# Third layer's experts: the order of the output additions, of the weight differences and of the small operations

## The chip, the cores and the metric

The kernel runs on one core of one Trainium2 chip. The metric is the device time of one launch in microseconds (us); the median of three runs stands for the kernel. Engines are called by the profile's names: PE is TensorE, DVE is VectorE, ACT is ScalarE, POOL is GpSimd, SP is the engine whose queue issues most of the DMAs.

## The reference, cut to what matters

The program is four layers on a picture of 256 channels and 64 x 64 positions (4096 tokens). The change lies in the end of the last layer, the mixture of experts:

```python
def _L3_ffn_ref(x, Wg, bg, W1, b1, W2, b2):
    xf = x.reshape(-1, D)
    gate_logits = xf @ Wg + bg
    top_w, top_i = jax.lax.top_k(gate_logits, TOP_K)
    top_w = jax.nn.softmax(top_w, axis=-1)
    w_dense = jnp.sum(jax.nn.one_hot(top_i, E, dtype=xf.dtype) * top_w[..., None], axis=1)
    out = jnp.zeros_like(xf)
    for e in range(E):
        h = jax.nn.gelu(xf @ W1[e] + b1[e], approximate=False)
        out = out + w_dense[:, e:e + 1] * (h @ W2[e] + b2[e])
    return out.reshape(B, L, D)
```

There are 8 experts, each token goes to 2 of them, the width is 256 and the hidden width 1024; everything is float32.

## The kernel before, in words

Tokens are sorted by expert into rows of a DRAM array `xs`, and the experts then work on tiles of 256 rows of one expert. `expert_tiles` (L2336) runs 36 such tiles, numbered 0 to 35 here. Tiles 0 to 19 (list "A") come from the first 3584 tokens and can start before the last block of 512 tokens has been routed; tiles 20 to 35 come from list "B".

Work of one tile *i*:

- `first` (L2373): the hidden layer. Eight products of 128 x 256 (`f_h_ps`, each four matmul records in the profile, so 32 a tile), each followed by a GELU on ACT (L2380). A PSUM buffer holds two products, and there are three of them, so a product can wait for an earlier GELU.
- `turn` (L2369): PE transposes the next tile's rows, DVE copies them (`f_xT`, L2308). The next tile's `first` needs them.
- `sums` (L2411): four DVE operations on halves of h (`f_hs`, L2419 to L2422). `sides` (L2400): four POOL operations on halves of the second weights (`f_wt`, L2408). Both feed a product by seven smaller products in place of eight (Strassen's scheme in Winograd's form).
- `second` (L2448) for the tile *before* (i - 1): `seven` (L2425) makes the seven products, first `ya`'s (two PSUM buffers) and `yb`'s (one), in the order ya, yb, yb, ya x3, yb. ACT copies one product (`f_u`, L2441), five DVE additions join them (L2442 to L2446), the sixth adds the bias (`f_y`, L2452), ACT multiplies by the router's weight (L2459, two operations), and POOL issues two indirect DMAs that scatter the rows to `ys` (L2460).
- `where` (L2396, with `expert_where`, L2287): eight or nine DVE operations of 128 x 2 elements (L2290 to L2301) that work out where tile i + 1's rows go and their weights. They are the "small operations" of the title.

Inside the loop, in the kernel before, the order of issue is: loads of later tiles (SP), `first`, `sides(i)`, hs[2], slot "hs", hs[0], `turn(i + 1)`, hs[1], hs[3], `where(i + 1)`, slot "turn", `second(i - 1)`, slot "end". The slots are filled from a table, `plan` (`put`, L2884): steps of the routing of the last block and of the tile list B, the check `limits3` (L2946), and for late tiles the reading back and transposing of finished output blocks. Each slot's step issues all that it holds on whatever engine: the layer norm of the last block (four DVE operations, L240, and a small POOL copy, L2055) at (2, "hs"), its transposes `part["turn"]` (L2057; PE, then an ACT or DVE copy, L2061) at (2, "turn") and (2, "end"), the logits (PE) at (3, "turn"), and so on.

What sets the order on each engine: while `written` (L2336, L2515) is in force, PE, DVE and POOL keep the order of the code (`manual_schedule`); ACT and SP are ordered by the library's scheduler with its own costs. When no entry of `plan` before tile 20 is left, only DVE keeps the code's order, and the scheduler orders PE and POOL too. In the kernel before this switch comes after tile 11 (its "hs" slot holds `limits`). I call tiles up to the switch "planned" and those after it "free".

The list A is made in `attn3` (L2580) near the end of the attention, in five steps of a generator `list_tiles` (L2120), spread over three of the attention's steps: `next(lists)` twice, twice and once (L2863 to L2868).

Of the kernel before, what the change touches and what calls it, by code (L numbers as in the profile page):

```python
# [26 lines left out]
TPB = NB // P  # L27
# [57 lines left out]
def bc(ap, axis, n):  # L85

    ap = ap.unsqueeze(axis)
    shape = list(ap.shape)
    shape[axis] = n
    return ap.to_broadcast(shape)  # L90


class Net:
# [2242 lines left out]
    def expert_tiles(self, S, order, wp, ps, early, pre, written):  # L2336
# [28 lines left out]
        def extra(i, slot):  # L2365
            for f in plan.pop((i, slot), ()):
                f()
# [32 lines left out]
        def sides(w2):  # L2400

            if L == 2:
                return None
            wt = wp.tile([P, 4, KH // 2, P], F32, tag="wt", name="f_wt", bufs=2)
            b = w2[:, : KH * C].rearrange("p (i m j n) -> p i m j n", i=2, j=2, n=P)
            for out, x, y in ((0, b[:, 0, :, 1], b[:, 0, :, 0]), (1, b[:, 1, :, 1], wt[:, 0]), (2, b[:, 1, :, 1], b[:, 0, :, 1]),
                              (3, b[:, 1, :, 0], wt[:, 1])):
                nc.gpsimd.tensor_tensor(wt[:, out], x, y, ALU.subtract)  # L2408
            return wt
# [12 lines left out]
                lambda: op(hs[:, 3], a[:, 1, :, 0], hs[:, 1], ALU.subtract),  # L2422
            )

        def seven(h, hs, w2, wt, y):  # L2425

            a = h.rearrange("p (i m) (j n) -> p i m j n", i=2, n=P)
            b = w2[:, : KH * C].rearrange("p (i m j n) -> p i m j n", i=2, j=2, n=P)

            pa = ps.tile([P, 4, P], F32, tag="ya", name="f_ya_ps", bufs=2)  # L2430
            pb = ps.tile([P, 4, P], F32, tag="yb", name="f_yb_ps")
            for out, x, z in (
                (pa[:, 0], a[:, 0, :, 0], b[:, 0, :, 0]), (pb[:, 2], a[:, 1, :, 0], b[:, 1, :, 0]), (pb[:, 1], a[:, 1, :, 1], wt[:, 3]),
                (pa[:, 2], hs[:, 0], wt[:, 0]), (pa[:, 1], hs[:, 1], wt[:, 1]), (pa[:, 3], hs[:, 2], wt[:, 2]), (pb[:, 0], hs[:, 3], b[:, 1, :, 1]),
            ):
                self.mm(out, [(x[:, m], z[:, m]) for m in range(KH // 2)])
            u1 = wp.tile([P, P], F32, tag="u1", name="f_u1")
            u2 = wp.tile([P, P], F32, tag="u2", name="f_u2")
            u = wp.tile([P, 2, P], F32, tag="u", name="f_u")
            flat = y.rearrange("p k (j n) -> p (k j) n", n=P)  # L2440
            nc.scalar.copy(u1, pa[:, 0])  # L2441
            nc.vector.tensor_tensor(flat[:, 0], u1, pb[:, 2], ALU.add)  # L2442
            nc.vector.tensor_tensor(u2, u1, pa[:, 1], ALU.add)
            nc.vector.tensor_tensor(u, pa[:, 2:4], bc(u2, 1, 2), ALU.add)
            nc.vector.tensor_tensor(flat[:, 3], u[:, 1], pa[:, 2], ALU.add)
            nc.vector.tensor_tensor(flat[:, 1:3], u, pb[:, 0:2], ALU.add)  # L2446

        def second(i, h, hs, w2, wt, at, wgt):  # L2448
            y = wp.tile([P, NI, C], F32, tag="y", name="f_y")
            if L == 3:  # L2450
                seven(h, hs, w2, wt, y)
                nc.vector.tensor_tensor(y, y, bc(w2[:, KH * C :], 1, NI), ALU.add)  # L2452
            else:
                p = ps.tile([P, NI, C], F32, tag="y", name="f_y_ps", bufs=2)
                for k in range(NI):
                    self.mm(p[:, k, :], [(h[:, m, k * P : (k + 1) * P], w2[:, m * C : (m + 1) * C]) for m in range(KH)])
                nc.vector.tensor_tensor(y, p, bc(w2[:, KH * C :], 1, NI), ALU.add)
            for k in range(NI):
                nc.scalar.mul(y[:, k, :], y[:, k, :], wgt[:, k : k + 1])  # L2459
                nc.gpsimd.indirect_dma_start(  # L2460
                    out=self.ys_parts[(i % 4) * NI + k], in_=y[:, k, :], in_offset=None,
                    out_offset=bass.IndirectOffsetOnAxis(ap=at[:, k : k + 1], axis=0),
                )
# [17 lines left out]
            to[0] = where(0, xs[0])  # L2481
        done = None
        free = not pre
        for i in tiles:
            if i + ahead_x <= tiles[-1]:
                xs[i + ahead_x] = rows(i + ahead_x)
            if i + ahead <= tiles[-1]:
                ws[i + ahead] = weights(i + ahead)
            w1, w2 = ws.pop(i)
            h = first(i, turned.pop(i), w1, not free)  # L2490
            hs, add = sums(h)
            now = (i, h, hs, w2, sides(w2)) + to.pop(i)
            for f in add[:1]:
                f()
            extra(i, "hs")
            for f in add[1:2]:
                f()
            if i < tiles[-1]:
                if i + 1 not in turned:
                    turned[i + 1] = turn(xs[i + 1])  # L2500
                for f in add[2:]:
                    f()
                to[i + 1] = where(i + 1, xs[i + 1])
                xs.pop(i)
            else:
                for f in add[2:]:
                    f()
            extra(i, "turn")
            if done is not None:
                second(*done)  # L2510
            extra(i, "end")
            done = now
            if not free and not any(k < pre["free"] for k, _ in plan):
                free = True
                written.close()  # L2515
                written.enter_context(self.tc.manual_schedule(engines={mybir.EngineType.DVE}))
# [63 lines left out]
    def attn3(self, t, S, out, limits):  # L2580
# [6 lines left out]
        with (  # L2587
# [28 lines left out]
            if True:  # L2616
# [230 lines left out]
                with tc.manual_schedule(engines={ET.PE, ET.Pool}):  # L2847
                    steps = iter(())
                    for g in range(first, G + LAG):
                        if g < G:  # L2850
                            scores(g)
                        values(g - LAG)
                        if g + 3 < G:
                            fetch(g + 3)
                        b, j = divmod(g - LAG, NPAIR)
                        if b > 0:
                            if j < TPB:
                                finish(b - 1, j)
                            elif j == TPB:
                                steps = routing((b - 1) * TPB, TPB, self.route)  # L2860
                            elif j % 2 == 0 or b == NBLK - 1:
                                next(steps, None)
                            if b == NBLK - 1 and j == TPB + 5:  # L2863
                                lists = self.list_tiles(S, keep, bank, "A", FULL)
                            if b == NBLK - 1 and j in (TPB + 5, TPB + 6):
                                next(lists)
                                next(lists)
                            if b == NBLK - 1 and j == TPB + 7:  # L2868
                                next(lists)
                                one = lambda shape, tag: keep.tile([P] + shape, F32, tag=tag, name="f_" + tag, bufs=1)  # L2870
                                tab = S["A"]["tab"], 0
                                pre = {"pool": keep, "x": self.expert_rows(*tab, one([NI, CX], "x")),
                                       "w": self.expert_weights(3, *tab, lambda: one([16 * P + 8], "w1"), lambda: one([9 * C], "w2"))}
                            if b == NBLK - 1 and j == NPAIR - 2:
                                pre["xT"] = self.expert_turn(pre["x"], bank().rearrange("p (k n) -> p k n", k=2), one([2, MT], "xT"))
                                tl = lambda tag, dt=F32: keep.tile([P, NI], dt, tag="e" + tag, name="f_" + tag, bufs=1)
                                pre["to"] = self.expert_where(S["A"], 0, pre["x"], tl)
# [10 lines left out]
                put(0, i, lambda i=i: (finish(last, i), part["stats"]([i])))  # L2888
            put(1, "turn", part["root"])
            put(2, "hs", part["scales"], part["norm"])  # L2890
            put(2, "turn", lambda: part["turn"](0))
            put(2, "end", lambda: part["turn"](1))
            put(3, "turn", part["logits"], part["top"], part["exp"])
            put(3, "end", part["weigh"], part["count"])
            put(4, "turn", part["place"], part["find"])
            put(4, "end", lambda: part["scatter"](range(2)))
            put(5, "end", lambda: part["scatter"](range(2, TPB)))
            put(5, "turn", go)
            put(6, "hs", go)
            put(7, "hs", go)  # L2900
            put(8, "hs", go)
            put(9, "turn", go)
            put(11, "hs", limits)
            ys = {}
            channels = out.rearrange("(m p) n -> p m n", p=P)

# [289 lines left out]
```

## Time and profile before

| what | us |
|---|---|
| median of three runs | 3430.52 |
| lowest, highest | 3427.38, 3432.81 |
| the profiled execution, its own time | 3429.62 |
| its span, first to last instruction | 3427.9 |
| planned tiles 2 to 12 (first matmul of tile 2 to that of tile 13) | 2884.68 to 3055.84: 171.16 |
| free tiles 13 to 30 | 3055.84 to 3314.57: 258.73 |
| tiles 31 to 35, with transposes of output among them | 3314.57 to 3392.99: 78.42 |

A tile's time is read off as the distance between the starts of its first `f_h_ps` matmul (from tile 31 on, of the output transpose that stands ahead of it) and that of the next tile. In the order of the tiles from 2 to 12 these are 19.75, 15.39, 14.04, 13.83, 13.60, 15.45, 14.89, 13.89, 13.60, 13.60 and 23.12 us; tiles 13 to 30 take 14.37 us each on average; 31 to 34 take 15.77 each and 35 takes 15.33. Times of the profile are microseconds from the start of the span. A line of the timeline has start, length, engine, line of the code, operation, what it writes and reads, shapes and count; in brackets stands the idle time of that engine just before, and who ended it.

### The profile page before, as it was taken

Reading aid. Unit: us, or ns where it says so; the run is one execution under the profiler, and the core shown is the slowest. Engines: PE = TensorE matmul, PEld = TensorE weight load, DVE = VectorE, ACT = ScalarE, POOL = GpSimd, SP = SyncE. Lnnn points to the kernel's source line nnn. Section 1 sums busy time; section 2 is a strip of 40 time slices with the busy share of each in tenths; the row PEclk is TensorE's granted clock in tenths of the full one; section 3 lists DMA queues with packets and bytes.
Section 4 is the critical chain, followed back from the end, with each engine's and each line's share of the span. In section 5 each row is a group of like instructions: output and inputs, shape, how many; then the busy total and the mean of one; then the engine's idle time right before and its main releaser. Section 6 shows DMA issues by size and latency. Waiting matters only on the chain. (4 is left out here: it accounts for less than half of the span.)

```text
span 3427.9 us, 66058 instructions
## 1 busy us (share of the span) xinstructions
PE 3111.8 (91%) x25682; PEld 2327.6 (68%) x25682; DVE 2353.5 (69%) x5332; ACT 1327.0 (39%) x2558; POOL 1455.1 (42%) x1316
## 2 busy tenths in 40 slices
PE   6779999999977899897959789999999999999997
PEld 3443444344436888666748667888888888988886
DVE  8885767577754677796646576777777776765564
ACT  4444344444425666243434353222222223323332
POOL 2028788788843555443434443000000013555552
PEclk9889999999989999998869899999999999999999
DMA  1145556521134222100129663233332234555564
GB/s 71 43 115 142 163 153 169 130 68 52 49 114 114 68 68 72 52 1 2 50 103 288 211 224 131 86 94 103 97 102 91 88 93 180 187 189 194 194 237 158
DMA packets 241689, 407.01 MB, mean 119 GB/s; under 512 B 78353, under 2 KB 152850, under 8 KB 231890
## 3 DMA queue, kind: packets, MB, share of 16 engines
q1 hardware_dynamic: 212866, 347.55, 32.6%
q0 software_dynamic: 13056, 35.93, 2.8%
q10 hardware_dynamic: 15440, 19.16, 1.7%
q8 instruction: 207, 3.39, 0.4%
q14 instruction: 120, 0.98, 0.1%
HBM read 287.07 MB, written 111.30 MB: 116 GB/s over the span
## 5 line engine op out<-in xcount | busy, mean ns | idle before, releaser
L776 ACT COPY l_sc<-l_s 128x384 f32<-128x384 f32 (+1 forms) x632 | 304.1, 533 | 453.5 <-PE l_s L769 442.4
L781 DVE TENSOR_TENSOR l_sm<-l_s,mask 128x256 f32<-128x256 f32 (+2 forms) x628 | 308.0, 552 | 89.8 <-PE l_s L769 88.7
L152 PE MATMUL f_h_ps<-f_xT,f_w 128*128 128x256 f32 x1440 | 345.5, 387 | 22.8 <-ACT f_h L2380 19.2
L2112 POOL DMA_INDIRECT xs<-f_room,f_to x64 | 64.4, 1007 | 644.0 <-DVE a_e L2737 476.9
L152 PEld LDWEIGHTS f_h_ps<-f_xT,f_w 128*128 128x128 f32 x1440 | 264.0, 191 | 82.5 <-ACT f_h L2380 32.7
L769 PE MATMUL l_s<-l_q,l_k 32*128 32x256 f32 (+3 forms) x2944 | 270.6, 453 | 0.0
L2769 ACT ACTIVATE a_e<-a_e 128x512 f32<-128x512 f32 x256 | 156.4, 631 | 250.2 <-DVE a_e L2739 229.2
L786 POOL TENSOR_TENSOR l_sm<-l_sc,mask 128x768 f32<-128x768 f32 (+1 forms) x116 | 202.6, 1754 | 87.8 <-ACT l_sc L776 87.7
L2460 POOL DMA_INDIRECT ys<-f_y,f_at x144 | 142.3, 988 | 193.6 <-ACT f_y L2459 144.4
L1156 DVE TENSOR_TENSOR l_pr<-l_vk,l_w_ps 128x1280 f32<-128x1280 f32 x128 | 186.7, 1483 | 54.3 <-PE l_acc_ps L1160 35.2
L2380 ACT ACTIVATE f_h<-f_h_ps,f_w 128x256 f32<-128x256 f32 x360 | 157.7, 469 | 164.0 <-PE f_h_ps L152 134.2
L769 PEld LDWEIGHTS l_s<-l_q,l_k 32*128 32x128 f32 x2944 | 132.5, 183 | 115.2 <-issue 66.8
L1160 PE MATMUL l_acc_ps<-ident,l_pr 128*128 128x128 f32 x1600 | 198.5, 278 | 6.3 <-POOL l_pr L1151 6.3
L1160 PEld LDWEIGHTS l_acc_ps<-ident,l_pr 128*128 128x128 f32 x1600 | 185.1, 144 | 12.9 <-POOL l_pr L1151 7.8
L790 POOL TENSOR_TENSOR l_sm<-l_sc,mask 128x256 f32<-128x256 f32 (+1 forms) x220 | 185.2, 871 | 14.6 <-ACT l_sc L776 13.9
L2408 POOL TENSOR_TENSOR f_wt<-f_w 128x512 f32<-128x512 f32 x72 | 93.3, 1310 | 187.9 <-PE f_ya_ps L152 158.4
L2750 PE MATMUL a_sa_ps<-a_q,a_kt 128*128 128x256 f32 x512 | 156.9, 388 | 17.8 <-DVE a_u L2755 15.9
L2754 ACT COPY a_u<-a_sa_ps 128x256 f32<-128x256 f32 x128 | 47.6, 372 | 292.4 <-PE a_sa_ps L2750 290.0
L2750 PE MATMUL a_sa_ps<-a_qt,a_kt 128*128 128x256 f32 x512 | 153.5, 382 | 0.0
L815 PE MATMUL l_b_ps<-l_sm,l_v 128*32 128x256 f32 (+2 forms) x2176 | 153.5, 372 | 0.0
L786 POOL TENSOR_TENSOR l_sm<-l_sc,mask_c 128x768 f32<-128x768 f32 (+1 forms) x64 | 121.0, 1906 | 39.8 <-ACT l_sc L776 39.2
L2789 PE MATMUL a_ob_ps<-a_et,a_vs 128*128 128x256 f32 x512 | 132.2, 381 | 0.0
(620 smaller groups left out, 7325.5 us busy)
## 6 DMA issues: line engine op xcount, KB each, us to landing
a_kt<-a_kd SPq DMA_DIRECT2D x128, 512.0 KB
f_w<-in_f_w SPq DMA_DIRECT2D x36, 1152.0 KB
f_w<-in_f_w SPq DMA_DIRECT2D x36, 1028.0 KB
xs<-zero SPq DMA_DIRECT2D x8, 4160.0 KB
l_vk<-vt SPq DMA_DIRECT2D x180, 128.0 KB
f_x<-xs SPq DMA_DIRECT2D x72, 260.0 KB
f_w<-in_f_w SPq DMA_DIRECT2D x36, 384.0 KB
l_rcp<-l_recd SPq DMA_DIRECT2D x48, 256.0 KB
```

The lines of the kernel that those rows point to most:

```text
L152: self.nc.tensor.matmul(out, lhsT, rhs, start=(i == 0), stop=(i == len(pairs) - 1))
L769: nc.tensor.matmul(s[pair, j][:, at : at + m, :], key(hp), qs[hp], start=(z == 0), stop=(z == len(pieces) - 1))
L776: nc.scalar.copy(sc[:, j], s[1, j])
L781: nc.vector.tensor_tensor(to(pair, j, kind, at), pick(s[pair, j], kind, which), mask, ALU.mult)
L786: nc.gpsimd.tensor_tensor(out[:, :, at, :], of[:, :, which, :], bc(mask, 1, 2), ALU.mult)
L790: nc.gpsimd.tensor_tensor(to(1, j, kind, at), pick(sc[:, j], kind, which), mask, ALU.mult)
L815: nc.tensor.matmul(out, pieces[z][1](hp), self.halves(sms[pair][:, j], wide)[:, of + skip * lo : of + skip * (hi - 1) + 1 : skip], start=n ...
L1156: nc.vector.tensor_tensor(pr, vk, bc(held["w"][:, j, dy], 3, D), ALU.mult)
L1160: nc.tensor.matmul(acc[:, m, j, :], pf[:, dx, m * P : (m + 1) * P], self.ident, is_transpose=True, start=(j == 0 and dy == 0 and dx == 0 a ...
L2380: nc.scalar.activation(h[:, m, :], p[:, m % 2, :], AF.Gelu, bias=w1[:, 2 * hidden + m : 2 * hidden + m + 1])
L2750: mm = lambda out, i, right: nc.tensor.matmul(out, A[i], right, start=True, stop=True)
L2769: nc.scalar.activation(e[:, i : i + 3 : 2], e[:, i : i + 3 : 2], AF.Exp, scale=1.0 / 16.0)
```

## The change

Three things are moved; no operation is added or removed.

1. In `seven`, the addition that reads `yb` (`flat[:, 0]`) comes after the two that read only `ya`.
2. The weight differences of tile i + 1 (`sides`) are issued inside `second(i - 1)`, right after its seven products, instead of those of tile i at the start of iteration i.
3. `where(i + 1)` comes right after hs[2] instead of after hs[3].

With them the plan is spread anew (steps come later, most by one tile), and the list A's steps are shared 3, 1, 1 instead of 2, 2, 1. The switch from planned to free now comes after tile 12.

```diff
-        def seven(h, hs, w2, wt, y):
+        def seven(h, hs, w2, wt, y, beside):
...
                 self.mm(out, [(x[:, m], z[:, m]) for m in range(KH // 2)])
+            beside()
...
             nc.scalar.copy(u1, pa[:, 0])
-            nc.vector.tensor_tensor(flat[:, 0], u1, pb[:, 2], ALU.add)
             nc.vector.tensor_tensor(u2, u1, pa[:, 1], ALU.add)
             nc.vector.tensor_tensor(u, pa[:, 2:4], bc(u2, 1, 2), ALU.add)
+            nc.vector.tensor_tensor(flat[:, 0], u1, pb[:, 2], ALU.add)
...
-            now = (i, h, hs, w2, sides(w2)) + to.pop(i)
+            now = (i, h, hs, w2, wts.pop(i)) + to.pop(i)
             for f in add[:1]:
                 f()
+            if i < tiles[-1]:
+                to[i + 1] = where(i + 1, xs[i + 1])
             extra(i, "hs")
             for f in add[1:2]:
                 f()
-            if i < tiles[-1]:
-                if i + 1 not in turned:
-                    turned[i + 1] = turn(xs[i + 1])
-                for f in add[2:]:
-                    f()
-                to[i + 1] = where(i + 1, xs[i + 1])
-                xs.pop(i)
-            else:
-                for f in add[2:]:
-                    f()
+            if i < tiles[-1] and i + 1 not in turned:
+                turned[i + 1] = turn(xs[i + 1])
+            for f in add[2:]:
+                f()
             extra(i, "turn")
-            if done is not None:
-                second(*done)
+
+            def beside():
+                if i < tiles[-1]:
+                    wts[i + 1] = sides(ws[i + 1][1])
+
+            if L == 2 or done is None:
+                beside()
+            if done is not None:
+                second(*done, beside)
...
-                                next(lists)
-                                next(lists)
+                                for _ in range(3 if j == TPB + 5 else 1):
+                                    next(lists)
...
-            put(2, "turn", lambda: part["turn"](0))
-            put(2, "end", lambda: part["turn"](1))
-            put(3, "turn", part["logits"], part["top"], part["exp"])
-            put(3, "end", part["weigh"], part["count"])
-            put(4, "turn", part["place"], part["find"])
-            put(4, "end", lambda: part["scatter"](range(2)))
-            put(5, "end", lambda: part["scatter"](range(2, TPB)))
-            put(5, "turn", go)
-            put(6, "hs", go)
+            put(2, "end", lambda: part["turn"](0))
+            put(3, "turn", lambda: part["turn"](1))
+            put(3, "end", part["logits"])
+            put(4, "hs", part["top"])
+            put(4, "turn", part["exp"])
+            put(5, "hs", part["weigh"], part["count"])
+            put(5, "turn", part["place"])
+            put(5, "end", part["find"], lambda: part["scatter"](range(2)))
+            put(6, "end", lambda: part["scatter"](range(2, TPB)))
+            put(6, "turn", go)
             put(7, "hs", go)
             put(8, "hs", go)
-            put(9, "turn", go)
-            put(11, "hs", limits)
+            put(9, "hs", go)
+            put(10, "turn", go)
+            put(12, "hs", limits)
```

`go` is one step of list B's generator, `limits` the check of `limits3`.

## The prediction

> **What bounds the kernel now.** I read the page's first parts (PE is 91% busy, clock 0.952), then PE's waits in the experts' stretch, then the timeline of single tiles. PE's own waits between 2870 and 3410 us:
>
> ```profile
> PE f_h_ps L152 <- ACT f_h L2380: 19.2, 24, 6.4
> PE tr_ps L251 <- ACTq L2333: 8.5, 1, 8.5
> PE f_h_ps L152 <- issue: 3.0, 3, 1.7
> PE a_q_ps L2060 <- DVE f_room L240: 2.9, 3, 1.0
> ```
>
> PE makes the tiles' pace, and it waits for the GELUs that free its PSUM buffers. Where it doesn't wait a tile takes 13.60 us (tiles 10 and 11). That is the floor; the timeline shows four kinds of excess over it.
>
> A free tile (its first matmul at T = 3199.58):
>
> ```profile
> 3198.94 2.50 POOL L2408 TENSOR_TENSOR f_wt<-f_w 128x512 f32<-128x512 f32 x2 [6.56 <-PE f_ya_ps L152]
> 3198.94 0.27 ACT L2441 COPY f_u<-f_ya_ps 128x128 f32<-128x128 f32 x1 [5.38 <-PE f_ya_ps L152]
> 3199.84 0.29 DVE L2442 TENSOR_TENSOR f_y<-f_u,f_yb_ps 128x128 f32<-128x128 f32 x1 [2.02 <-PE f_yb_ps L152]
> 3200.04 0.28 DVE L2443 TENSOR_TENSOR f_u<-f_u,f_ya_ps 128x128 f32<-128x128 f32 x1
> ...
> 3201.39 2.94 POOL L2408 TENSOR_TENSOR f_wt<-f_w,f_wt 128x512 f32<-128x512 f32 x2
> 3201.47 1.74 DVE L2452 TENSOR_TENSOR f_y<-f_y,f_w 128x512 f32<-128x512 f32 x1
> ...
> 3203.25 0.91 ACT L2459 ACTIVATE f_y<-f_y,f_wgt 128x256 f32<-128x256 f32 x2 [1.26 <-DVE f_y L2452]
> ...
> 3204.06 1.19 ACT L2380 ACTIVATE f_h<-f_h_ps,f_w 128x256 f32<-128x256 f32 x3
> ```
>
> The additions wait for `yb`, though ya's copy was done 0.6 us before. The bias addition takes 1.74 us where it took 0.69 elsewhere: it starts 0.08 us after POOL's third difference, and has to let that pass. ACT's multiplications come after it, the next GELU behind them in ACT's queue, and PE gets its buffer at T + 4.99:
>
> ```profile
> 3218.94 2.86 PE L152 MATMUL f_h_ps<-f_xT,f_w 128*128 128x256 f32 x12 [0.49 <-ACT f_h L2380]
> ```
>
> (the next tile, T = 3213.95). The brackets' 0.49 is less than the loss, since the matmul before is still draining: 14.37 - 13.60 = 0.77 us a tile. From tile 31 the same wait is larger.
>
> Tile 2, where PE transposes rows whose norm isn't ready:
>
> ```profile
> 2890.09 5.98 DVE L240 TENSOR_SCALAR f_room<-t,ln_mv,ln_rstd 128x256 f32<-128x256 f32 x4
> ```
>
> Four operations take 1.5 us each, beside POOL's differences (2890.76 to 2895.9). Tile 12, the first free one:
>
> ```profile
> 3032.27 1.23 DVE L2290 TENSOR_SCALAR f_first<-f_x,f_exA 128x2 f32<-128x2 f32 x1
> 3033.53 1.19 DVE L2291 TENSOR_SCALAR f_second<-f_first 128x2 f32<-128x2 f32 x1
> 3034.75 1.19 DVE L2292 TENSOR_TENSOR f_wgt<-f_second,f_x 128x2 f32<-128x2 f32 x1
> ...
> 3042.30 0.91 ACT L2459 ACTIVATE f_y<-f_y,f_wgt 128x256 f32<-128x256 f32 x2 [7.17 <-DVE f_y L2452]
> ```
>
> Here POOL does two tiles' differences in a row (3028.83 to 3039.71) and the small operations take 1.2 us each instead of 0.16; additions, multiplications and GELUs follow late, PE waits 6.39 us and goes on at a lower clock. Tiles 7 and 8 lose 1.85 and 1.29 us likewise: list steps on DVE, stretched by POOL, make `f_xT` late.
>
> **What the Trainium skill says.** "SBUF — State Buffer", section "Who interferes with whom": VectorE and GpSimd share one pair of SBUF ports, locked for a whole instruction; a VectorE operation with two SBUF inputs, and copies and tensor_scalar in a two-port mode, block against GpSimd; one with at most one SBUF input outside these modes doesn't. The trace agrees: additions that read PSUM (L2442 to L2446) keep their 0.28 to 0.42 us beside the differences, the bias addition waits. "PSUM — Partial Sum Buffer", section "Engine vs sequencer instructions": the queues of ScalarE, VectorE and GpSimd are strict FIFO; so the GELU behind the waiting multiplications in the trace. "TensorE: Matmul & The Clock Gate", section "What's actually happening": an idle PE loses clock. Agrees: after the 6.39 us gap twelve matmuls take 5.49 us instead of 2.86.
>
> **The change, part by part.** On each engine the order of the changed program is as the diff says: in free tiles ACT and POOL keep theirs and DVE alone differs; in planned tiles ACT multiplies after the first GELU instead of the second, and POOL's differences stand ahead of the scatter DMAs.
>
> *Additions.* With ya's last product at T - 0.64 and the copy's 0.27, the first two additions run between about T - 0.3 and T + 0.4; `yb`'s follow in its own time. From the spacings in the trace (u to the next 0.46 or 0.33, then 0.21, 0.20, 0.45) the bias addition starts near T + 1.2, now T + 1.89. POOL's differences begin at T - 0.64, 1.23 us each: operations end at T + 0.59, T + 1.83, T + 3.06. So the bias addition takes the port at T + 1.83, ends near T + 2.45 instead of T + 3.63, multiplications end at T + 3.4, the GELU PE needs at T + 3.8; PE is there at T + 4.32 (20 x 0.216). The stall goes: 18 free tiles x 0.77 = 13.9. What is late next is the GELUs' chain behind PE, 0.3 to 0.5 us clear of it. If the port is missed once more, nothing is gained: bounds 0 and 13.9; I take 13.9, since the margin is 0.6 us.
>
> *Tiles 31 to 35.* ACT's output copy (0.59 us) now stands behind the multiplications, and PE needs the second GELU: copy at T + 3.3, GELUs from T + 3.83, second done at T + 4.66 (0.36 apart, 0.47 long), against PE ready at T + 4.41 and today's T + 5.35. Left 0.29 of 0.94: 5 x 0.65 = 3.3 (0 to 4.7). The output DMA on SP now stands behind the weights' load; nobody waits for it.
>
> *Planned tiles and the plan.* The differences run from T - 0.64 to T + 4.9 in every tile, the scatter DMAs to T + 7.2, and nothing on POOL until the next tile. DVE: hs[2] ends near T + 5.6, small operations (now 1.7) to T + 7.4, steps in the slot "hs" behind, hs[0] needs the last GELU (T + 7.9), then `f_xT` 1.3 us later; PE needs that at T + 13.6. A step may thus take some 4 us. The longest, the choice of the top two and the fourth of list B, have 14 to 16 operations of about 0.2: 3 us. Norm: four operations of at most 0.7 where no POOL operation runs beside them; its transposes now come at the tile's end, about 4 us later than needed. So tiles 2 to 12 should take 11 x 13.60 = 149.6 plus PE's moved work, which stays: two times four transposes 0.44 each, logits 1.70, place 0.37, lists 0.17 and 0.16: 3.28 together. 152.9 against 171.16: 18.3 gained (tile 2: 5.7, which is what its 6.15 of excess leaves when one transpose step of 0.44 stays; tile 12: 9.5; tiles 7 to 9: 3.4; the rest is moved between tiles). I take 0.8 off for seams of 0.07 as tiles 3 to 5 show.
>
> The differences need a tile's second weights sooner: loaded behind the bias addition two tiles ahead, 24 us before; the slowest first load took 9.9 us (issued 2861.71, used 2871.56). Hidden. In tile 0 the small operations fall beside POOL's differences (2871.56 to 2877): delayed at most 6 us, hs[0] at 2878.3, used by PE at 2881.1. Hidden too, 2.8 us clear.
>
> *An unknown:* small operations now lie beside POOL's indirect DMAs. One row speaks to it:
>
> ```profile
> 2969.41 0.96 POOL L2460 DMA_INDIRECT ys<-f_y,f_at  x1 [0.30 <-ACT f_h L2380]
> 2969.67 2.07 DVE L2169 TENSOR_SCALAR f_pick<-count,f_pair 128x64 f32<-128x64 f32 x1
> 2970.40 1.28 POOL L2408 TENSOR_TENSOR f_wt<-f_w 128x512 f32<-128x512 f32 x1
> ```
>
> It waits through the DMA as well. Bounds: 0, or until T + 7.2, so 2 us on DVE, which has over 4 us to spare. I take 0 for the end.
>
> *List A's steps* (3, 1, 1): as many DVE operations among the attention's, moved by 0.1 to 0.5 us; PE waits there 1.04 us for an exponential's input that these do not set. 0, bounds -0.5 and +1. The last tile's additions start before `yb`: 0.4 gained at the end.
>
> Sum: 13.9 + 3.3 + 17.5 + 0.4 = 35.1. Against the profiled execution's 3429.62 (1.7 over its span): 3394.5. The median is 0.9 above that execution: **3395.4**.
>
> **Rivals.** *Only the plan pays (10%):* the free tiles keep 0.77, if the bias addition still misses POOL's boundary. For: it is missed now by 0.08 only. Against: it comes 0.6 us sooner. 3430.5 - 17.9 = 3412.6. *Only the additions pay (7%):* the plan's stalls move with it, a step in "hs" ahead of hs[0] makes `f_xT` late. For: that is what happened in tiles 7 and 8. Against: POOL is done by then. 3430.5 - 17.6 = 3412.9. *Slower (4%):* POOL's indirect DMAs hold the port against every small operation. If these take 7.7 us as in tile 12 (3032.27 to 3039.92), they end at T + 13.3, `f_xT` is ready at T + 14.6 and the additions start a further 1.3 later, so GELUs stall PE again: 14.6 + 0.7 = 15.3 a tile, 18 x 0.93 = 17 lost, planned tiles 11 x 1.7 = 19 lost of the 18.3 to be gained, tiles 31 to 35 5 lost: about 3453. It decides from 6.5 us of small operations a tile; two DMAs give 2. *Hardly any change (3%):* part of each, within 7 us of 3430.5.
>
> **How the numbers follow.** The forecast has 76%, with a range of its own from 3390 (all of tiles 31 to 35, 1 us in the attention, no seams) to 3402 (a fifth of both gains lost). To leave out no more than 2 in 10 the range takes in the two partial rivals and goes to 3413. Faster by over 0.2% (6.9 us, what a measurement of this kernel can tell from none) 93%, within 3%, slower 4%.
>
> **What would show it.** Right: tiles of 13.6 in both parts; the bias addition near T + 1.2 and of 1.2 us; no wait of PE on L2380 outside tiles 31 to 35; L240 at 0.7 or less; no gap at the switch. Wrong: L2452 still at 1.7, small operations of 1 us beside L2460, or PE idle at a tile's start.

## The result and the profile after

The median went from 3429.19 to 3398.24 us (four runs each; 3427.38 to 3432.81 and 3391.79 to 3402.67). The ratio is 0.9907, with a 95% interval of 0.9888 to 0.9926: faster by 0.9%, inside the range on record, 2.8 us above the forecast. The profiled execution after took 3399.46 us, its span 3397.7; the one before 3429.62 and 3427.9. By stages, from the starts of the tiles in the two traces (forecast as the prediction summed it):

| stage | before | after | difference | forecast |
|---|---|---|---|---|
| up to tile 2 | 2884.68 | 2885.92 | +1.24 | 0 |
| tiles 2 to 12 | 171.16 | 156.93 | -14.23 | -17.5 |
| tiles 13 to 30 | 258.73 | 245.10 | -13.63 | -13.9 |
| tiles 31 to 35 | 78.42 | 74.74 | -3.68 | -3.3 |
| after them | 34.91 | 35.01 | +0.10 | -0.4 |
| sum | 3427.9 | 3397.7 | -30.2 | -35.1 |

PE's own waits in the experts' stretch (total, times, longest), to be held against the four lines shown of before:

```profile
PE tr_ps L251 <- ACTq L2333: 7.8, 1, 7.8
PE a_q_ps L152 <- DVE f_both L2085: 1.1, 1, 1.1
PE a_q_ps L152 <- DVE f_cum L2094: 0.3, 1, 0.3
PE f_h_ps L152 <- issue: 0.2, 1, 0.2
```

The 24 waits for a GELU (19.2 us) are gone, and so is the wait for the norm. One wait is new: for `f_both` and `f_cum`, two results of the routing's count. A free tile in the profile after (its first matmul at T = 3233.48):

```profile
3232.84 2.50 POOL L2408 TENSOR_TENSOR f_wt<-f_w 128x512 f32<-128x512 f32 x2 [5.41 <-PE f_ya_ps L152]
...
3234.20 0.42 DVE L2447 TENSOR_TENSOR f_y<-f_u,f_yb_ps 128x256 f32<-128x256 f32 x1
3234.60 0.47 ACT L2380 ACTIVATE f_h<-f_h_ps,f_w 128x256 f32<-128x256 f32 x1 [1.49 <-PE f_h_ps L152]
3234.65 1.24 DVE L2453 TENSOR_TENSOR f_y<-f_y,f_w 128x512 f32<-128x512 f32 x1
...
3235.30 3.06 POOL L2408 TENSOR_TENSOR f_wt<-f_w,f_wt 128x512 f32<-128x512 f32 x2
...
3235.92 0.91 ACT L2460 ACTIVATE f_y<-f_y,f_wgt 128x256 f32<-128x256 f32 x2
3236.73 0.90 ACT L2380 ACTIVATE f_h<-f_h_ps,f_w 128x256 f32<-128x256 f32 x2
```

The bias addition (now L2453) starts at T + 1.17, inside GpSimd's second difference, and ends at T + 2.41, 0.55 us after that difference does (3235.34). Now it is the third difference that waits: the second pair takes 3.06 us where the first took 2.50. The multiplications end at T + 3.35, the GELU behind them at T + 3.72, and PE, due at T + 4.3, doesn't wait. The next tile starts 13.62 us later.

The norm of the last block (L240), which lies in tile 2:

```profile
2893.21 1.38 DVE L240 TENSOR_SCALAR f_room<-t,ln_mv,ln_rstd 128x256 f32<-128x256 f32 x4 [0.23 <-DVE ln_rstd L228]
```

1.38 us for four operations instead of 5.98. The tiles from 2 to 12 now take 14.04, 15.74, 13.68, 17.46, 13.83, 13.59, 13.97, 13.60, 13.82, 13.60 and 13.60 us. One of them stands out, tile 5:

```profile
2937.95 0.41 PE L152 MATMUL a_q_ps<-f_both,before 128*128 128x32 f32 x2 [1.06 <-DVE f_both L2085]
2938.64 0.41 PE L152 MATMUL a_q_ps<-f_cum,all_one 128*128 128x32 f32 x2 [0.28 <-DVE f_cum L2094]
2938.88 1.23 PE L152 MATMUL f_ya_ps<-f_w,f_h 128*128 128x128 f32 x8
2939.90 1.92 PE L152 MATMUL f_yb_ps<-f_w,f_h 128*128 128x128 f32 x8
2941.62 1.82 PE L152 MATMUL f_yb_ps<-f_wt,f_h 128*128 128x128 f32 x8
2943.27 2.84 PE L152 MATMUL f_ya_ps<-f_wt,f_hs 128*128 128x128 f32 x24
```

PE stands still for 1.34 us at the place products, and then groups of eight products take 1.92 and 1.82 us instead of 1.06. In the windows view the granted clock (the column before the DMA share) is halved in that stretch:

```profile
2939.90:2943.20 3.30, 3.30 (x18) 3.30 (x17) 1.38 (x3) 0.00 (x0) 0.00 (x0) 0.50 0.31 126
2943.30:2947.00 3.70, 3.70 (x35) 3.70 (x34) 0.46 (x2) 0.27 (x1) 0.80 (x1) 1.00 0.00 0
```

### The profile page after: what moved, and what is told of

Read it like the earlier page. It is cut to its first block, busy times and chain, and to the rows that moved or that the text cites. A ratio compares the mean times of both kernels' runs of the same rounds, so it can differ in the third digit from the quotient of the medians.

```text
span 3397.7 us, 66019 instructions
## 1 busy us (share of the span) xinstructions
PE 3103.7 (91%) x25682; PEld 2327.4 (68%) x25682; DVE 2323.7 (68%) x5332; ACT 1330.4 (39%) x2558; POOL 1462.3 (43%) x1316
## 5 line engine op out<-in xcount | busy, mean ns | idle before, releaser
L152 PE MATMUL f_h_ps<-f_xT,f_w 128*128 128x256 f32 x1440 | 338.0, 384 | 0.9 <-issue 0.4
L2461 POOL DMA_INDIRECT ys<-f_y,f_at x144 | 148.9, 1034 | 124.4 <-ACT f_y L2460 75.7
L1160 PEld LDWEIGHTS l_acc_ps<-ident,l_pr 128*128 128x128 f32 x1600 | 184.7, 144 | 14.2 <-POOL l_pr L1151 8.5
```

What stands on the lines that cost most here:

```text
L152: self.nc.tensor.matmul(out, lhsT, rhs, start=(i == 0), stop=(i == len(pairs) - 1))
L1160: nc.tensor.matmul(acc[:, m, j, :], pf[:, dx, m * P : (m + 1) * P], self.ident, is_transpose=True, start=(j == 0 and dy == 0 and dx == 0 a ...
```

## The experiments

The theory: the additions' order alone makes the gain of the free tiles, the differences' place that of the planned tiles. The rivals: the small operations or the new plan do it. The runs were made in three sets (e1 to e4, e5 to e8, e9 and e10). The layers ahead of the experts took some 40 us less in the first and third set than in the second (the kernel before: 3388.36, 3427.38, 3386.34); why isn't known. So whole times are compared within a set only. The stages carry the reading: in the two executions of the change they differ by less than 0.1 us. Of the kernel before there is one trace, that of the first comparison, and all stages are held against it:

| kernel | tiles 2 to 12 | 13 to 30 | 31 to 35 | ratio to before, interval |
|---|---|---|---|---|
| before | 171.16 | 258.73 | 78.42 | |
| the change | 156.93 | 245.10 | 74.74 | 0.9907 (0.9888 to 0.9926) |
| e8, the change again | 156.85 | 245.10 | 74.72 | 0.9921 (0.9905 to 0.9938) |
| e1, additions alone | 170.49 | 245.11 | 74.71 | 0.9938 (0.9921 to 0.9955) |
| e2, change, old additions | 156.63 | 257.94 | 78.39 | 0.9956 (0.9941 to 0.9970) |
| e3, change, old differences | 173.32 | 249.57 | 74.71 | 0.9964 (0.9950 to 0.9978) |
| e4, change, old plan | 154.27 | 245.10 | 74.73 | 0.9907 (0.9890 to 0.9923) |
| e5, change, old small operations | 153.68 | 245.11 | 74.73 | 0.9913 (0.9897 to 0.9930) |
| e6, change, later place products | 153.15 | 245.38 | 74.73 | 0.9914 (0.9898 to 0.9931) |
| e7, before, halved differences | 169.99 | 245.10 | 73.69 | 0.9962 (0.9948 to 0.9976) |
| e9, additions and differences alone | 153.16 | 245.10 | 74.73 | 0.9894 (0.9877 to 0.9910) |
| e10, e6 with halved differences | 155.25 | 245.38 | 73.10 | 0.9902 (0.9886 to 0.9919) |

The ratios bear the stages out only roughly. In the second set the medians give 4 to 8 us less than the stages add up to; for e7 it is 11.9 us against 19.5, which lies outside the interval. The time ahead of tile 2, which e7's edit doesn't reach, differs between the traces (2884.68 before; 2885.25 to 2891.80 in that set), and this covers part of it. The stages say what an edit does to the tiles; that each such gain arrives whole in the total isn't shown.

**e1, the additions alone.** In the kernel before:

```diff
-            nc.vector.tensor_tensor(flat[:, 0], u1, pb[:, 2], ALU.add)
             nc.vector.tensor_tensor(u2, u1, pa[:, 1], ALU.add)
             nc.vector.tensor_tensor(u, pa[:, 2:4], bc(u2, 1, 2), ALU.add)
+            nc.vector.tensor_tensor(flat[:, 0], u1, pb[:, 2], ALU.add)
```

> The kernel before with one part of the change alone: the addition that reads yb stands behind the two that read only ya. My theory: this alone makes the free tiles' gain, because the bias addition comes to the shared port one difference of GpSimd earlier. Free tiles 13.62 instead of 14.37 us, bias addition near T + 1.2 and about 1.25 us long, tiles 31 to 35 near 15.0, PE's waits for the GELUs of L2380 gone from the free tiles; planned tiles as before, within 1 us of 171.2 together. Time: 3429.2 - 13.6 - 3.7 = 3412. The rival: in the free tiles it is the place of the small operations, or what the scheduler makes of the new order, that counts; then free tiles stay at 14.37 and the time at 3429.

The free tiles took 13.62 us and their stage fell by 13.6, the last tiles' by 3.7. The planned tiles gained 0.7. The bias addition, in a tile with T = 3193.39:

```profile
3194.55 1.24 DVE L2452 TENSOR_TENSOR f_y<-f_y,f_w 128x512 f32<-128x512 f32 x1
```

The rival that gives this gain to the small operations or to the scheduler is out: the small operations stand where they stood, and in the free tile compared (number 20) PE, ACT and POOL have the order of the kernel before; DVE alone differs.

**e2, the change with the old order of additions** (the two lines of e1 the other way round).

> The changed kernel with the additions in their old order. My theory: free tiles go back to 14.37 us (13.6 lost), tiles 31 to 35 to 15.7 (3.7 lost), and the planned tiles, in which GpSimd's differences now lie beside the additions too, lose as well, up to 0.77 each (8.5): 3398.2 + 17 to 26 = 3415 to 3424. Rival one, the planned tiles don't care, because ScalarE multiplies there behind the first GELU: 3415. Rival two, the additions' order matters only with the old place of the small operations: 3398.

The free tiles went back to 14.37 us, all but the first of them (tile 13, 13.62), and the last ones to 15.77; the planned tiles lost nothing (156.63). So rival one has the number. Its reason wasn't put to the test, since in the planned tiles the bias addition hardly waits: 0.69 us in most, 1.07 at most. A free tile and a planned tile of this kernel, GpSimd's differences and the bias addition in each:

```profile
3182.49 2.50 POOL L2408 TENSOR_TENSOR f_wt<-f_w 128x512 f32<-128x512 f32 x2 [6.56 <-PE f_ya_ps L152]
...
3184.95 2.94 POOL L2408 TENSOR_TENSOR f_wt<-f_w,f_wt 128x512 f32<-128x512 f32 x2
3185.02 1.75 DVE L2453 TENSOR_TENSOR f_y<-f_y,f_w 128x512 f32<-128x512 f32 x1
```

```profile
2883.23 1.26 POOL L2408 TENSOR_TENSOR f_wt<-f_w 128x512 f32<-128x512 f32 x1 [6.89 <-PE f_ya_ps L152]
2884.57 1.27 POOL L2408 TENSOR_TENSOR f_wt<-f_w,f_wt 128x512 f32<-128x512 f32 x1
2885.76 0.69 DVE L2453 TENSOR_TENSOR f_y<-f_y,f_w 128x512 f32<-128x512 f32 x1
2885.79 1.79 POOL L2408 TENSOR_TENSOR f_wt<-f_w 128x512 f32<-128x512 f32 x1
```

In the free tile the third difference begins 0.07 us ahead of the bias addition, which then takes 1.75. In the planned tile the second difference starts 1.34 us after the first instead of 1.23, the bias addition is 0.03 us ahead of the third, and takes 0.69; it is the difference that grows, to 1.79. A tenth of a microsecond decides who waits. Where that tenth comes from stands in the lines: in the code's order the second difference reads what the first has just written (`f_wt<-f_w,f_wt`), while in the free tiles the scheduler puts the two that read only `f_w` first. In all the traces with whole differences, one that reads the result just before it starts 1.33 to 1.37 us after it, the others 1.22 to 1.26, where VectorE holds neither up.

**e3, the change with the differences in their old place** (`sides(w2)` where `wts.pop(i)` stands, nothing in `beside`).

> The changed kernel with the weight differences back in their old place, those of a tile at its own start in the order of issue; additions, small operations and the new plan stay. My theory: the differences beside the norm, the list steps and the small operations are what stretched the planned tiles. Some of the 14.2 us comes back: the switch (now after tile 12) has GpSimd make two tiles' differences in a row again, 5 to 9.5 us there, and the list steps lose 1 to 4: 3404 to 3411. Rival: the plan's new spread alone cures the planned tiles, since the steps have later due times: 3398. Free tiles are the scheduler's and stay at 13.62 in either case.

Tiles 2 to 12 took 173.32 us, 16.4 more than in the change, and tile 13, the first after the switch, 18.09 instead of 13.62: 20.9 lost, more than the 6 to 13 expected, and more than the kernel before takes there. Without the differences' move, the new plan and the small operations' new place together are no cure but a loss. PE's waits in these tiles:

```profile
PE a_q_ps L152 <- DVE f_both L2085: 5.7, 1, 5.7
PE f_h_ps L152 <- issue: 3.3, 3, 2.2
PE f_h_ps L152 <- ACT f_h L2380: 2.4, 1, 2.4
PE a_q_ps L152 <- DVE f_room L2061: 1.6, 1, 1.6
```

The wait for `f_both` of tile 5 is there again, and now 5.7 us (tile 5 takes 23.35 us): the small operations ahead of the count run beside GpSimd's differences, and four of the eight take 1.12 to 2.01 us each.

**e4, the change with the old plan** (the `put` lines of before).

> The changed kernel with the old plan (each routing step one tile or half a tile earlier, and the switch from planned to free after tile 11). My theory: with the differences out of the way the old plan does nearly as well, the norm's four operations take 0.4 us each, but its transposes, due half a tile after it, are late by some 2 us with clock loss behind it, and steps of tile 3 likewise: 2 to 8 us lost: 3400 to 3406. Rival: the new spread is where the gain of the planned tiles comes from; then 12 to 14 us are lost: 3410 to 3412.

Both theories fall: nothing was lost, and the tiles 2 to 12 took 2.7 us *less* than with the new plan. Tile 5 takes 13.83 us instead of 17.46, and tile 4, where the place products lie now, 14.05. Tile 2 takes 15.58, since the transposes wait for the norm:

```profile
2859.55 1.29 PE L2060 MATMUL a_q_ps<-ident,f_room 128*128 128x128 f32 x4 [0.25 <-DVE f_room L240]
```

The bracket shows the wait ahead of the first one alone. The four take 1.29 us instead of 0.60, and the product behind them begins 1.11 us later in the tile than in e9, where the norm is done in time; that is all of the difference between the two tiles (15.58 and 14.47).

**e5, the change with the small operations back behind hs[3]**:

```diff
-            if i < tiles[-1]:
-                to[i + 1] = where(i + 1, xs[i + 1])
             extra(i, "hs")
...
             for f in add[2:]:
                 f()
+            if i < tiles[-1]:
+                to[i + 1] = where(i + 1, xs[i + 1])
             extra(i, "turn")
```

> The changed kernel with the small operations back behind hs[3]. My theory: their move buys nothing by itself, and it costs: in tile 5 it puts 1.6 us of them ahead of the count of the experts, whose result PE's place products wait for (1.06 and 0.28 us, and slow products after them). So tile 5 falls from 17.46 to about 14.0, all other tiles stay, tiles 2 to 12 take 153.4 instead of 156.9. Rival: the small operations behind hs[3] fall onto the next tile's additions or the steps of the slot before them, and the tiles with steps grow by 0.5 to 1 us each: 158 to 162.

153.68 us, as expected; tile 5 takes 14.25. In its trace the count comes right behind hs[2], and the place products follow PE's transposes with no wait:

```profile
2934.36 0.69 DVE L2419 TENSOR_TENSOR f_hs<-f_h 128x512 f32<-128x512 f32 x1 [3.13 <-ACT f_h L2380]
2934.97 0.16 DVE L2017 TENSOR_SCALAR top_w<-top_e 128x4 f32<-128x4 f32 x1
...
2935.46 0.18 DVE L2085 TENSOR_TENSOR f_both<-f_hot 128x32 f32<-128x32 f32 x1
...
2936.05 0.31 PE L152 MATMUL a_q_ps<-f_both,before 128*128 128x32 f32 x2
```

So the small operations' move does harm here: 1.6 us of them ahead of a step on which PE waits.

**e6, the place products at the end of tile 5:**

```diff
-            put(5, "turn", part["place"])
-            put(5, "end", part["find"], lambda: part["scatter"](range(2)))
+            put(5, "end", part["place"], part["find"], lambda: part["scatter"](range(2)))
```

> The changed kernel with one step of the plan later: the place products of tile 5 from the slot behind the next tile's transposes to the tile's end. My theory: tile 5's excess is PE's wait for the count on VectorE (1.34 us) and the lower clock after it (about 1.9 us over 32 products), so both go and only the products' own 0.37 stays: tile 5 near 14.0, tiles 2 to 12 near 153.4. Rival: the products themselves, or something else in tile 5, are slow; or at the end of the tile they wait again and make the next tile late: tiles 5 and 6 together stay at 31.3.

Tile 5 takes 13.97 us and tile 6 13.90, together 27.9 instead of 31.3. With the same products at another moment the excess is gone, and nowhere in these tiles is the granted clock halved, so it was the wait and the clock behind it. (Tile 13 takes 0.28 us more here, 13.90; why wasn't followed.)

**e7, before with halved differences:**

```diff
-                nc.gpsimd.tensor_tensor(wt[:, out], x, y, ALU.subtract)
+                for v in (slice(0, KH // 4), slice(KH // 4, KH // 2)):
+                    nc.gpsimd.tensor_tensor(wt[:, out, v], x[:, v], y[:, v], ALU.subtract)
```

> The kernel before, with each of GpSimd's four differences made as two operations of half the size; nothing else. My theory: the bias addition is slow because it has to let one whole operation of GpSimd pass, so with operations half as long it waits half as long: it ends near T + 3.1 instead of T + 3.6, and free tiles fall from 14.37 to 13.6 to 13.9 (9 to 14 us of the whole), although the additions keep their order. Rival: the two engines slow each other down in proportion for as long as both run, or it is the additions' late start alone that counts: the bias addition stays at 1.7 us or grows, since GpSimd is busy longer, and free tiles at 14.37 or more.

Free tiles took 13.62 us and the last ones 14.83 with the *old* order of additions. The number is the theory's, but not by its way. Two halves take longer than a whole difference (1.37 us from pair to pair instead of 1.23), so the third pair begins at T + 2.10 instead of T + 1.82. The bias addition, at T + 1.89 as ever, now falls ahead of it, as in the planned tile of e2, and takes 0.80 (T = 3195.75 here):

```profile
3196.48 1.40 POOL L2409 TENSOR_TENSOR f_wt<-f_w,f_wt 128x256 f32<-128x256 f32 x2
...
3197.64 0.80 DVE L2453 TENSOR_TENSOR f_y<-f_y,f_w 128x512 f32<-128x512 f32 x1
...
3197.85 1.85 POOL L2409 TENSOR_TENSOR f_wt<-f_w 128x256 f32<-128x256 f32 x2
```

So e7 shows again that it counts who comes first. That a shorter operation on the other side makes the wait shorter can't be read from it: whole differences of 1.37 us would have done the same. e10 shows that.

**e8, the change once more.**

> The changed kernel once more, as the measure for the other three on the same chip: tiles 2 to 12 at 156.9, free tiles at 13.62, tiles 31 to 35 at 15.04; over the kernel before as measured, a ratio of 0.991.

The stages came out the same. Against it, in the same set, e5 took 3.9 us less and e6 3.5 (medians 3396.65 and 3397.11 against 3400.59), as their stages say (3.2 and 3.4); the intervals overlap, so it is the stages that show it.

**e9, additions and differences alone** (the change without the small operations' move, with the old plan and the list A's old steps).

> The kernel before with two parts alone: the additions' order and the weight differences beside them. Small operations, plan and the list A's steps stay as they were. My theory now: these two make the whole gain, and the move of the small operations and the new spread of the plan bring nothing. Tiles 2 to 12 at 154 (as with the old plan and the moved small operations, 154.27), tile 2 near 15.6, tile 12 at 13.6; free tiles 13.62. Over the kernel before: 16.9 + 13.2 + 3.7 = 34 us less, a ratio near 0.990. Rival: the small operations' move is needed with the differences, because behind hs[3] they delay the steps of the slot that follows: tiles 2 to 4 lose 1 us each: 157 or more.

Tiles 2 to 12 took 153.16 us, 3.8 less than in the change, tile 2 14.47. All of the gain is in these two parts; the others give some back. The ratio, 0.9894, is the best of all, though its interval overlaps the change's. Why tile 2 needs no later transposes:

```profile
2848.76 1.25 POOL L2461 DMA_INDIRECT ys<-f_y,f_at  x1 [0.15 <-issue]
...
2849.33 1.41 DVE L240 TENSOR_SCALAR f_room<-t,ln_mv,ln_rstd 128x256 f32<-128x256 f32 x4
2850.31 0.96 POOL L2461 DMA_INDIRECT ys<-f_y,f_at  x1 [0.30 <-issue]
```

With no small operations ahead of it the norm is done at 2850.7, before PE's transposes (2851.07), and the scatter DMAs of GpSimd beside it cost it next to nothing (1.41 us against 1.38 in the change).

**e10, e6 with halved differences.**

> The changed kernel with the place products at the end of tile 5 and with GpSimd's four differences made as eight of half the size. From the runs with one of these each: tiles 2 to 12 near 153.2, free tiles 13.62 (nothing left to gain), tiles 31 to 35 at 14.4 to 14.8 instead of 15.04, because the bias addition waits less for the port and the GELUs behind it come sooner: 4 to 6 us less than the changed kernel, a ratio to the kernel before of 0.990. Rival: GpSimd's eight operations take 5.6 to 6.5 us instead of 4.9 to 5.6 and push its scatters onto the small operations and hs[2]: the planned tiles grow by 0.2 to 0.5 each and the gain is gone.

The last tiles took 14.7 us, 1.6 less for the stage, as expected. The bias addition of a free tile (T = 3094.54) starts at T + 1.16, as in the change:

```profile
3095.70 0.84 DVE L2454 TENSOR_TENSOR f_y<-f_y,f_w 128x512 f32<-128x512 f32 x1
```

It takes 0.84 us instead of 1.24: the half difference under way ends at T + 1.4, where a whole one ended at T + 1.86. Here the shorter operation does shorten the wait. But tile 8 took 15.70, 2.1 more, which undoes it; what happened there is new and stands in the last section.

## Why the prediction was right, and where it was off

In the traces the gain is 4.9 us short of the sum (30.2 for 35.1); that the median missed by only 2.8 is luck. The forecast added 0.9 us because the profiled execution before lay that far under its median, and the one after happened to lie 1.2 above its own.

*Additions, free tiles* (-13.9): right in size and mechanism. e1 makes it alone, e2 undoes it, and e7 makes it from the other side, by a third difference that comes later than the addition. The bounds 0 and 13.9 were fair: the miss before was 0.08 us (e2: 0.07).

*Tiles 31 to 35* (-3.3): 3.7. The tile's gain is 0.73 instead of 0.65, and it needs the additions alone (e1).

*The differences beside the additions.* Tiles 2 to 12 went from 170.49 (e1) to 153.16 (e9) by this part alone: -17.3, where the sum had 17.5 for the differences, the plan and the small operations together. So 152.9 plus some seams was the right floor, and the norm, the switch and the list steps were what kept the tiles above it.

*The step that failed* is "A step may thus take some 4 us". It measured the room by when `f_xT` is due (T + 13.6). The place products aren't bound by that: in PE's written order they stand behind the transposes, at T + 7.5 (2936.9), and their operand, `f_both`, was finished at T + 8.5 (2937.9), because the small operations now ran ahead of it. It takes the new plan as well: with the old one (e4) the products lie in tile 4, which took 14.05 us, as in e9. The prediction counted these products as 0.37 us of work and gave their wait nothing. It cost 1.34 us of standing still and some 1.7 of half clock after it: the next three groups begin 1.02, 1.72 and 1.65 us apart where 0.89 is usual. e5 and e6 each take it away, and with it 3.2 and 3.7 us of tiles 2 to 12. This is nearly all that the planned tiles lack (17.5 - 14.2 = 3.3).

*The plan's new spread and the small operations* were not parts with a gain. With the old plan the move of the small operations costs 1.1 us (e4 against e9, in tile 2); the new spread costs 0.5 without that move (e5 against e9) and 2.7 with it (the change against e4). Against e9 the list A's steps differ too, but they lie ahead of tile 2.

*The unknown of GpSimd's indirect DMAs*: taken as 0, and in effect it was. In the tiles 2 to 12 after the change the small operations, most of them beside L2461, take 0.15 to 0.31 us. L2169, which took 2.07 us in the kernel before, takes 0.26 beside such a DMA after the change, and 0.40 in e5 and e9. In the kernel before a difference came right behind the DMA, and L2169 ended just after that (2971.74 and 2971.68). But it had started 0.7 us ahead of the difference; why it didn't get through in that time isn't shown.

*The rest.* The attention's steps (0 forecast): from the list's count products to the first hidden product it took 33.05 us with the old steps (e1, e9) and 33.31 with the new (e2, e3, e4, e10) in the first and third set, so some 0.26 more. In the other runs it took 35.0 with the old (before, e7) and 34.3 (the change, e8) or 35.0 (e5, e6) with the new. Nothing is gained there for certain, and the steps weren't tried by themselves. The 1.24 us by which tile 2 starts later come from ahead of the change: list A's count products were already 1.96 us later. The 0.4 at the end wasn't seen.

*The rivals.* "Only the additions pay" was near in one point, that a step in "hs" becomes late; but it was late for PE's own products and not for `f_xT`, and in one tile out of eleven. "Slower" needed 6.5 us of small operations a tile; there were 1.8 at most from the first to the last.

## What to carry to other kernels

Where two engines share a lock that is held for a whole instruction, look in the trace at which one starts first and by how little: where the two starts are within a tenth of a microsecond, an addition that comes 0.7 us sooner, or another order or size of the operations on the other side, was worth 5% of a tile here. When a step is given a later slot, check it against each engine that keeps a written order: room before the tile's last deadline says nothing about a matmul that stands in the middle of PE's queue. And try the parts of a change one by one: here two of them made all of the gain and the rest cost 3.8 us.

## What the runs showed of the hardware that was not expected

A wait of 1.06 and one of 0.28 us, with four transposes and four small products around them, were enough for PE's granted clock to fall to 0.50 for 3.4 us (2939.79 to 2943.21). The fall comes about 2 us after PE has resumed (2937.95); in e2 the same wait is followed by slow products from the first group on (1.77, 1.92, 1.29 us for eight). The Trainium skill, "TensorE: Matmul & The Clock Gate", section "What's actually happening", puts the fall after an idle window of some 3.4 us; no single wait of this tile is that long, so either shorter gaps add up or the window is judged otherwise. The clock as the traces record it says a little more. In every trace it is 1.00 or 0.50, and all falls of one execution lie on one grid of 3.41 us (to 0.01 us) and last a whole multiple of that, but for the last, which the end of the trace cuts. That fits with the fall coming 1.8 us after PE has resumed in the change and 1.25 us after it in e2. In the 3.41 us ahead of it PE was busy for 2.07 us in the change, 2.07 in e8 and 2.00 in e2. But busy time alone doesn't decide: 1.48 us in the kernel before (from 3035.74) and 1.57 in tile 8 of e10 (from 2933.79) were followed by a full clock. What else counts is open.

An operation of VectorE that waits for the port doesn't always get it at GpSimd's next boundary. In tile 8 of e10 the bias addition begins 0.03 us after a difference and takes 4.67 us, against 0.84 in the tiles around it: it lets all six half differences that are left pass.

```profile
2929.75 1.41 POOL L2409 TENSOR_TENSOR f_wt<-f_w,f_wt 128x256 f32<-128x256 f32 x2
2929.78 4.67 DVE L2454 TENSOR_TENSOR f_y<-f_y,f_w 128x512 f32<-128x512 f32 x1
2930.60 0.47 ACT L2380 ACTIVATE f_h<-f_h_ps,f_w 128x256 f32<-128x256 f32 x1 [2.35 <-PE f_h_ps L152]
2931.12 1.40 POOL L2409 TENSOR_TENSOR f_wt<-f_w 128x256 f32<-128x256 f32 x2
2932.49 1.40 POOL L2409 TENSOR_TENSOR f_wt<-f_w,f_wt 128x256 f32<-128x256 f32 x2
```

In e7 one bias addition of 36 (tile 7) took 3.60 us and let four further halves pass. With whole differences none took over 1.75, one operation's wait. Why the boundaries between halves are sometimes not enough is open; it makes short operations on the other side a gamble, for 1.6 us gained in e10 and 2.1 lost.
